# A Mamba block's convolution moved from diagonal matmuls to stacked, DMA-shifted copies on column tiles

## The chip, the cores and the metric

The kernel runs on one core of a Trainium2 chip. The core has five engines that work side by side, each through its own queue in program order: PE (TensorE, matmuls), DVE (VectorE), ACT (ScalarE), POOL (GpSimd) and SP (SyncE, which here only issues DMA transfers). The metric is the device time of one execution, in microseconds (us); lower is better.

## The reference

8192 rows x of 512 columns pass through two residual blocks. c and wmod give shift, scale and gate of each (sa, ca, ga, sb, cb, gb).

```python
h = _layernorm(x) * (1 + ca) + sa
xc, z = split(h @ W_in.T)                       # 1024 columns each
xc = silu(conv(xc, W_conv))                     # per column: 4 taps over the last 4 rows
dlt, Bm, Cm = split(xc @ W_xproj.T)             # 32, 16 and 16 columns
delta = softplus(dlt @ W_dt.T + b_dt)
# for each of 1024 columns d and 16 states n, over the 8192 rows in order:
s = exp(delta * A[d, n]) * s + delta * Bm[n] * xc[d];   y[d] += s * Cm[n]
x = x + ga * (((y + xc * D) * silu(z)) @ W_out.T)
h = _layernorm(x) * (1 + cb) + sb
x = x + gb * fp4_linear(silu(fp4_linear(h, w_gate)) * fp4_linear(h, w_up), w_down)
```

fp4_linear rounds both operands to a 4-bit grid, with one scale for each 16 values. All is float32.

## The kernel before

The rows are cut into 16 chunks of 512 (T), the 1024 inner columns into 8 blocks of 128 (ND), two blocks making one of four h groups. In the Mamba part columns lie on the partitions and rows run along the free axis.

**The scan loop.** The work is cut into 1024 slots: 16 chunks of 64 slots, one slot being one block and two states (`unit`, from L546). For each slot POOL multiplies delta times x by the rows of B into db (`make_db`, L521, two slots ahead), ACT takes the exponential into da (`make_da`, L534, one slot ahead, in PSUM), DVE runs the recurrence over 1024 elements (L559) and multiplies the result by the rows of C into hc (L577), or, in 5 of 16 slots, the scan writes hp and POOL does that product (L572). PE transposes the result into y (`add_up`, L438). Buffers: three db, two da, two hc and two hp.

**The rows of B and C** of two states, spread over all partitions, come by `load_bc` (L515): at the start of every second slot SP issues one 512 KB load of B and one of C, for the pair of slots that begins four slots later. Each has three buffers, so the load of C waits until the product with the rows three pairs back is done.

**The order of the rest** is written out by hand. `TABLE` (L589) gives for each step of chunk k a time in quarter-slots, counted from the chunk's first slot; a negative one lies in the chunk before. A quarter is one of four moments in `unit`: BEGIN (ahead of the slot), MID (between the two halves of da), GAP (ahead of make_db) and END. Every engine meets the work in this order, SP included. The convolution of chunk k thus runs during the slots of chunk k-1, in 15 passes (a few steps reach further back). Chunk 0's own convolution stands in the prologue, in steps called halves (L857 to L864, `on(h, ...)`), beside the FP4 quantization of w_gate and w_up, whose results go to DRAM.

**The convolution of one block d** has six steps:
- `conv_mm` (L285): four matmuls, 128x128 weights from w_in (the whole of W_in, resident in SBUF) against the normalized rows hT, into a PSUM tile cv;
- `conv_raw` (L297): ACT copies cv to raw, behind three carried columns, and keeps the last three for the next chunk;
- `conv_diag` (L290): ACT makes four diagonal 128x128 matrices, the identity times one tap each;
- `conv_taps` (L305): four matmuls of these against raw at four shifts, added up in cv;
- `conv_act` and `conv_out` (L312, L315): ACT takes tanh, DVE forms the block of xc.

cv comes from a pool of one PSUM bank in the loop, shared with the transposes of the norm (L267) and one of the two delta matmuls of a group. `x_proj` then makes 64 rows: 32 for delta, 16 of B, 16 of C; B and C go to DRAM for load_bc (L342). `prep_mm` (L358) makes delta of a group's two blocks from the 32 rows, one matmul of 32x128 weights each; `prep` is its softplus.

**The FFN** comes after the loop and shares only x and the quantized weights with it.

Of the kernel before, what the change touches and what calls it, by code (L numbers as in the profile page):

```python
# [108 lines left out]
def mamba_then_fp4_ffn(  # L109
# [60 lines left out]
    with ExitStack() as ma:  # L170
# [5 lines left out]
        cw = wp.tile([P, ND, 4], F32, tag="cw", name="cw")  # L176
# [8 lines left out]
        w_in = wi.tile([P, NK, 2 * DI], F32, tag="w_in", name="w_in")  # L185
        w_xp = wi.tile([P, ND, RK + 2 * NS], F32, tag="w_xp", name="w_xp")
        w_dt = wi.tile([RK, DI], F32, tag="w_dt", name="w_dt")
# [90 lines left out]
        def in_proj(k, o, ps):  # L278
            for f in range(NK):
                nc.tensor.matmul(  # L280
                    ps, lhsT=w_in[:, f, o : o + P], rhs=hT[k][:, f, :],
                    start=(f == 0), stop=(f == NK - 1),
                )

        def conv_mm(k, d):  # L285
            v = cv_tile(f"cv_{k}_{d}")
            in_proj(k, d * P, v)
            pend["v", k, d] = v

        def conv_diag(k, d):  # L290

            taps = s1.tile([P, 4, P], F32, tag="taps", name=f"taps_{k}_{d}")
            for i in range(4):
                nc.scalar.activation(taps[:, i, :], ident, AF.Copy, scale=cw[:, d, i : i + 1])  # L294
            pend["taps", k, d] = taps

        def conv_raw(k, d):  # L297
            v = pend["v", k, d]
# [4 lines left out]
            pend["raw", k, d] = raw  # L303

        def conv_taps(k, d):  # L305
            v, raw, taps = pend["v", k, d], pend["raw", k, d], pend.pop(("taps", k, d))
            for i in range(4):
                nc.tensor.matmul(  # L308
                    v, lhsT=taps[:, i, :], rhs=raw[:, i : i + T], start=(i == 0), stop=(i == 3)
                )  # L310
# [10 lines left out]
        def x_proj(k, half):  # L321
# [3 lines left out]
            for d in range(half * (ND // 2), (half + 1) * (ND // 2)):  # L325
                nc.tensor.matmul(
                    pb[: RK + 2 * NS, :], lhsT=w_xp[:, d, :], rhs=xcs[k, d],
# [9 lines left out]
        def x_proj_out(k, _=None):  # L337
            pb = pend.pop(("pb", k))
            dbc = s1.tile([RK + 2 * NS, T], F32, tag="dbc", name=f"dbc_{k}")
            nc.scalar.activation(dbc, pb[: RK + 2 * NS, :], AF.Copy)  # L340
            bc = scr.tile([2 * NS, T], F32, tag="bc", name=f"bc_{k}")
            nc.sync.dma_start(bc, dbc[RK:, :])  # L342
            dbcs[k], bcd[k], pend["pb", k] = dbc, bc, pb

        def first_mm(k, _=None):

            nc.tensor.matmul(
                pend["pb", k][:, :NS], lhsT=dbcs[k][:, 0:1].to_broadcast([RK + 2 * NS, P]),
                rhs=ident[: RK + 2 * NS, RK : RK + NS], start=True, stop=True,
# [8 lines left out]
        def prep_mm(k, h):  # L358
            for i in range(DH):
                d = h * DH + i  # L360
                pd = mm_tile(f"pd_{k}_{d}") if i % 2 else cv_tile(f"pd_{k}_{d}")
# [904 lines left out]
```

## Time and profile before

| | us |
|---|---|
| runs: median of 2 (lowest to highest) | 5705.88 (5698.72 to 5713.04) |
| profiled execution: span, first to last instruction | 5691.5 |
| until the first scan | 161 |
| scan loop, 161 to 3770 | 3609 |
| after it, the FFN | 1921.5 |

The profiled execution's own time outside its span is not listed; the median of the runs lies 14.4 us above its span.

How to read the lines: engine, source line, operation, then the tiles written and read; "x" is a count; then busy time and mean duration, or, in lines ordered by time, the start, the length and (in brackets) the idle time just before with what ended it. PE's float32 matmul of 128x512 appears as two records. In the list of waits a line has the waiting instruction, what it waited for, the sum in us, how often, and the longest. SPq is SP's queue of transfers, "to landing" the time from issue to the data's arrival.

### The profile page before, as it was taken

What the parts mean: (1) busy time and instruction counts of PE and PEld (TensorE: products, weight loads), DVE (VectorE), ACT (ScalarE), POOL (GpSimd) and SP (SyncE); (2) the same over time, 40 slices, a digit from 0 to 9 for tenths busy, and PEclk for the clock granted to TensorE, in tenths of its full rate; (3) what the DMA queues carried; (4) which work ended last, traced back from release to release, by engine and by line L of the source; (5) the groups of instructions that cost most, each with busy time, mean ns of one, the idle gap of its engine ahead of it and who ended that gap; (6) DMA issues with size and microseconds to landing.
All of it is one profiled execution on the core that took longest, in us unless ns stands there. A gap on an engine that the chain in (4) does not pass through costs nothing. (4 is left out here: it accounts for less than half of the span.)

```text
span 5691.5 us, 59773 instructions
## 1 busy us (share of the span) xinstructions
PE 5218.3 (92%) x19844; PEld 3065.0 (54%) x19844; DVE 4956.7 (87%) x4003; ACT 3214.2 (56%) x7319; POOL 4047.2 (71%) x2548
## 2 busy tenths in 40 slices
PE   7789889899899898998998988778999999999999
PEld 4556556556665565665666655543444444444444
DVE  7899999999999999999999999999687788878885
ACT  6677787777777777777777776643122222221221
POOL 4899999999999999999999999983222232223320
PEclk9899999999999999999999999889999999999999
DMA  5444454454445444544445444440100000000000
GB/s 183 150 158 157 156 160 162 154 169 153 161 154 164 153 161 156 163 163 160 157 158 160 155 160 151 160 165 17 34 27 23 27 31 32 23 24 31 33 13 15
DMA packets 221996, 659.50 MB, mean 116 GB/s; under 512 B 24915, under 2 KB 40403, under 8 KB 221686
## 3 DMA queue, kind: packets, MB, share of 16 engines
q1 hardware_dynamic: 221110, 654.63, 35.3%
q8 instruction: 156, 2.56, 0.2%
q14 instruction: 154, 1.26, 0.1%
q10 hardware_dynamic: 576, 1.05, 0.0%
HBM read 615.22 MB, written 40.38 MB: 115 GB/s over the span
## 5 line engine op out<-in xcount | busy, mean ns | idle before, releaser
L521 POOL TENSOR_TENSOR db<-bc,du 128x1022 f32<-128x1022 f32 x1024 | 2388.8, 2357 | 25.1 <-DVE da L559 20.9
L559 DVE TENSOR_TENSOR_SCAN da<-da,db 128x1024 f32<-128x1024 f32 x704 | 1610.0, 2287 | 100.3 <-ACT da L534 87.4
L534 ACT ACTIVATE da<-delta,na 128x512 f32<-128x512 f32 x2048 | 1412.4, 690 | 90.4 <-DVE hp L559 62.3
L577 DVE TENSOR_TENSOR hc<-da,bc 128x1024 f32<-128x1024 f32 x704 | 861.3, 1223 | 88.6 <-PE y L438 38.7
L438 PE MATMUL y<-ident,hc 128*128 128x128 f32 x5632 | 767.9, 287 | 154.1 <-DVE hc L577 98.3
L438 PEld LDWEIGHTS y<-ident,hc 128*128 128x128 f32 x5632 | 674.9, 148 | 330.5 <-issue 158.2
L97 POOL TENSOR_TENSOR xn<-xn,sc 128x1536 f32<-128x1536 f32 (+2 forms) x80 | 201.2, 2515 | 865.4 <-DVE xn L92 857.3
L559 DVE TENSOR_TENSOR_SCAN hp<-da,db 128x1024 f32<-128x1024 f32 x320 | 730.0, 2281 | 51.0 <-ACT da L534 45.3
L572 POOL TENSOR_TENSOR hp<-hp,bc 128x1024 f32<-128x1024 f32 x320 | 754.2, 2357 | 25.6
L1060 PE MATMUL pu<-xqT,wu 128*128 128x512 f32 x1408 | 637.3, 595 | 6.2 <-DVE ve L32 3.6
L1060 PE MATMUL pg<-xqT,wg 128*128 128x512 f32 x1408 | 638.1, 596 | 2.9 <-ACT g L1065 2.2
L83 ACT ACTIVATE a<-xn 128x512 f32<-128x512 f32 (+3 forms) x144 | 145.7, 1012 | 862.7 <-DVE xn L79 832.9
L1094 PE MATMUL po<-wd,hT 128*128 128x512 f32 x1408 | 608.7, 593 | 2.0 <-DVE hT L1080 2.0
L280 PE MATMUL cv<-hT,w_in 128*128 128x512 f32 x1024 | 490.2, 624 | 32.9 <-ACT hT L273 16.1
L412 PE MATMUL pz<-w_in,hT 128*128 128x256 f32 x2048 | 495.4, 398 | 26.6 <-DVE z L427 21.6
L308 PE MATMUL cv<-raw,taps 128*128 128x512 f32 x1024 | 469.3, 601 | 5.4 <-ACT taps L294 5.1
L474 PE MATMUL po<-w_o,xc 128*128 128x512 f32 x1024 | 457.4, 592 | 0.2 <-ACT xc L467 0.2
L412 PEld LDWEIGHTS pz<-w_in,hT 128*128 128x128 f32 x2048 | 404.1, 202 | 95.3 <-DVE z L427 26.0
L1060 PEld LDWEIGHTS pu<-xqT,wu 128*128 128x128 f32 x1408 | 267.9, 191 | 342.2 <-issue 323.2
L1094 PEld LDWEIGHTS po<-wd,hT 128*128 128x128 f32 x1408 | 267.9, 190 | 339.8 <-issue 330.6
L557 ACT ACTIVATE state<-da 128x2 f32<-128x2 f32 x703 | 118.0, 168 | 588.7 <-DVE hc L577 586.9
L1060 PEld LDWEIGHTS pg<-xqT,wg 128*128 128x128 f32 x1408 | 266.6, 191 | 327.3 <-issue 319.8
(125 smaller groups left out, 6696.6 us busy)
## 6 DMA issues: line engine op xcount, KB each, us to landing
bc<-bc SPq DMA_DIRECT2D x1024, 512.0 KB, 4.3
x<-in_x_dram SPq DMA_DIRECT2D x64, 256.0 KB, 4.7
h<-in_x_dram SPq DMA_DIRECT2D x64, 256.0 KB, 2.8
x<-mo SPq DMA_DIRECT2D x64, 256.0 KB, 2.9
out_dram<-x SPq DMA_DIRECT2D x64, 256.0 KB, 2.0
mo<-po SPq DMA_DIRECT2D x60, 256.0 KB, 2.2
w_in<-in_w_inT_dram SPq DMA_DIRECT2D x2, 2048.0 KB, 9.8
wm<-in_wmod_dram SPq DMA_DIRECT2D x8, 512.0 KB, 4.5
```

The costliest lines, as they stand in the source:

```text
L280: nc.tensor.matmul(ps, lhsT=w_in[:, f, o : o + P], rhs=hT[k][:, f, :], start=(f == 0), stop=(f == NK - 1),)
L308: nc.tensor.matmul(v, lhsT=taps[:, i, :], rhs=raw[:, i : i + T], start=(i == 0), stop=(i == 3))
L412: nc.tensor.matmul(pz[:, b, :], lhsT=hT[k][:, f, t0 : t0 + P], rhs=w_in[:, f, o : o + DH * P], start=(b == 0 and f == 0), stop=(f == NK - ...
L438: nc.tensor.matmul(y[:, j, i * P : (i + 1) * P], lhsT=src[:, j * P : (j + 1) * P], rhs=ident, start=start and j % 2 == 0, stop=stop, is_tr ...
L474: nc.tensor.matmul(pend["po", k, j], lhsT=xcs[k, d][:, j * P : (j + 1) * P], rhs=w_o[:, d, :], start=(d == 0), stop=(d == ND - 1),)
L521: nc.gpsimd.tensor_tensor(db[:, :, 1:], bct[slot // DH, 0][:, :, 1:], dus[k, h, i][:, 1:].unsqueeze(1).to_broadcast([P, GN, T - 1]), ALU.mult,
L534: nc.scalar.activation(pend["da", slot][:, q, :], deltas[k, h][:, i, :], AF.Exp, scale=na[:, d, n : n + 1])
L559: nc.vector.tensor_tensor_scan(flat(to), flat(da), flat(db), 0.0, ALU.mult, ALU.add)
L572: nc.gpsimd.tensor_tensor(to, to, c_rows, ALU.mult)
L577: nc.vector.tensor_tensor(hc, hs, c_rows, ALU.mult)
L1060: nc.tensor.matmul(ps, lhsT=wt[:, k, f * P : (f + 1) * P], rhs=xqT[n][:, k, :], start=(k == 0), stop=(k == NK - 1),)
L1094: nc.tensor.matmul(pos[j], lhsT=hTs[n, c][:, o : o + P], rhs=wd[:, f0 + i, :], start=(f0 + i == 0), stop=(f0 + i == NF - 1),)
```

## The change

The four shifts are no longer taken by reading raw at four offsets on PE. `conv_raw` now also issues 16 transfers from SBUF to SBUF, each 32 partitions of 512 values: shift i of the 32-column group g goes to partitions 32i to 32i+31 of a tile rows. `conv_taps` then needs one matmul for each group of 32 columns, with weights of 128x32 that hold four 32x32 diagonals, each on its own column tile of PE and into its own 32 partitions of a fresh cv tile. These weights (taps) are made once, by DVE in `neg_a`, and `conv_diag` is gone. cw is loaded by 16 small transfers in the order that this needs.

The half of W_in for x is not resident any more: `load_w` brings 128 columns (256 KB) for each block, into two buffers. The delta rows are made twice (w_xp has 96 columns), and the two delta matmuls of a group stand on two row tiles (partitions 0 to 31 and 32 to 63).

In the compiled instruction lists each of the 16 copies waits on SP for the transfer issued eight transfers earlier to have landed, as other transfers did before; nothing else on SP is reordered, the loads of B and C stay where they were. Times of the convolution's steps in TABLE change as shown; all other times stay.

```diff
-        cw = wp.tile([P, ND, 4], F32, tag="cw", name="cw")
+        taps = wp.tile([P, ND, 4, 32], F32, tag="taps", name="taps")
...
-        w_in = wi.tile([P, NK, 2 * DI], F32, tag="w_in", name="w_in")
-        w_xp = wi.tile([P, ND, RK + 2 * NS], F32, tag="w_xp", name="w_xp")
-        w_dt = wi.tile([RK, DI], F32, tag="w_dt", name="w_dt")
+        w_z = wi.tile([P, NK, DI], F32, tag="w_z", name="w_z")
+        w_xp = wi.tile([P, ND, 2 * RK + 2 * NS], F32, tag="w_xp", name="w_xp")
+        w_dt = wi.tile([2 * RK, ND // 2, P], F32, tag="w_dt", name="w_dt")
+        wxp = ma.enter_context(tc.tile_pool(name="wx", bufs=2))
...
+        def load_w(k, d):
+            wx = wxp.tile([P, NK, P], F32, tag="wx", name=f"wx_{k}_{d}")
+            nc.sync.dma_start(
+                wx, w_inT[:, d * P : (d + 1) * P].rearrange("(k p) n -> p k n", p=P)
+            )
+            pend["wx", k, d] = wx
...
-        def conv_diag(k, d):
-
-            taps = s1.tile([P, 4, P], F32, tag="taps", name=f"taps_{k}_{d}")
-            for i in range(4):
-                nc.scalar.activation(taps[:, i, :], ident, AF.Copy, scale=cw[:, d, i : i + 1])
-            pend["taps", k, d] = taps
-
         def conv_raw(k, d):
-            v = pend["v", k, d]
+            v = pend.pop(("v", k, d))
             raw = s2.tile([P, T + 3], F32, tag="raw", name=f"raw_{k}_{d}")
             nc.scalar.activation(raw[:, 3 : T + 3], v, AF.Copy)
             nc.scalar.activation(raw[:, 0:3], tail[:, d, :], AF.Copy)
             nc.scalar.activation(tail[:, d, :], v[:, T - 3 : T], AF.Copy)
-            pend["raw", k, d] = raw
+
+            rows = s1.tile([P, 4, T], F32, tag="rows", name=f"rows_{k}_{d}")
+            for i in range(4):
+                for g in range(4):
+                    nc.sync.dma_start(
+                        rows[32 * i : 32 * (i + 1), g, :], raw[32 * g : 32 * (g + 1), i : i + T]
+                    )
+            pend["raw", k, d], pend["rows", k, d] = raw, rows
 
         def conv_taps(k, d):
-            v, raw, taps = pend["v", k, d], pend["raw", k, d], pend.pop(("taps", k, d))
-            for i in range(4):
+            v = pend["v", k, d] = cv_tile(f"cx_{k}_{d}")
+            rows = pend.pop(("rows", k, d))
+            for g in range(4):
                 nc.tensor.matmul(
-                    v, lhsT=taps[:, i, :], rhs=raw[:, i : i + T], start=(i == 0), stop=(i == 3)
+                    v[32 * g : 32 * (g + 1), :], lhsT=taps[:, d, g, :], rhs=rows[:, g, :],
+                    start=True, stop=True, tile_position=(0, 32 * g),
                 )
...
+                r = slice(i * RK, (i + 1) * RK)
                 nc.tensor.matmul(
-                    pd, lhsT=w_dt[:, d * P : (d + 1) * P], rhs=dbcs[k][:RK, :], start=True, stop=True
+                    pd, lhsT=w_dt[r, h, :], rhs=dbcs[k][r, :], start=True, stop=True,
+                    tile_position=(i * RK, 0),
                 )
...
             "conv": (
-                (-251, -247, -246, -242, -231, -229), (-228, -221, -220, -213, -207, -205),
-                (-201, -196, -191, -188, -184, -182), (-174, -170, -164, -162, -159, -149),
-                (-139, -133, -130, -128, -122, -120), (-119, -114, -113, -108, -105, -97),
-                (-89, -85, -81, -78, -71, -66), (-59, -58, -55, -54, -49, -46),
+                (-290, -251, -247, -233, -231, -229), (-262, -228, -222, -209, -207, -205),
+                (-231, -201, -196, -182, -180, -178), (-203, -173, -169, -154, -152, -149),
+                (-174, -139, -133, -122, -120, -118), (-140, -116, -112, -100, -98, -96),
+                (-119, -91, -87, -70, -68, -66), (-88, -63, -60, -42, -40, -38),
             ),
...
-            "conv": (conv_mm, conv_raw, conv_diag, conv_taps, conv_act, conv_out),
+            "conv": (load_w, conv_mm, conv_raw, conv_taps, conv_act, conv_out),
...
-                nc.vector.tensor_scalar(cw, cw, 0.5, None, ALU.mult)
+                fold = mp.tile([P, 32], F32, tag="fold", name="fold")
+                nc.vector.tensor_reduce(
+                    fold, ident.rearrange("p (b c) -> p c b", c=32), AX.X, ALU.add
+                )
+                nc.vector.scalar_tensor_tensor(
+                    taps.rearrange("p d g c -> p (d g) c"),
+                    cw.rearrange("p d g -> p (d g)").unsqueeze(2).to_broadcast([P, 4 * ND, 32]),
+                    0.5, fold.unsqueeze(1).to_broadcast([P, 4 * ND, 32]), ALU.mult, ALU.mult,
+                )
...
-            nc.sync.dma_start(w_in[:, :, :DI], w_inT[:, :DI].rearrange("(k p) n -> p k n", p=P))
-            nc.sync.dma_start(cw, w_conv)
+            load_w(0, 0)
+            load_w(0, 1)
+            cw = mp.tile([P, ND, 4], F32, tag="cw", name="cw")
+            for i in range(4):
+                for g in range(4):
+                    nc.sync.dma_start(
+                        cw[32 * i : 32 * (i + 1), :, g], w_conv[32 * g : 32 * (g + 1), :, i]
+                    )
...
                 on(h, conv_mm, 0, d)
                 on(h + 1, conv_raw, 0, d)
-                on(h + 1, conv_diag, 0, d)
+                on(h, load_w, 0, d + 2) if d + 2 < ND else None
                 on(h + 2, conv_taps, 0, d)
```

## The prediction

> **What bounds the kernel now.** I read the page's first part, then busy time by stage, then the waits of the engines that are nearly full. The page:
>
> ```profile
> span 5691.5 us, 59773 instructions
> ...
> PE 5218.3 (92%) x19844; PEld 3065.0 (54%) x19844; DVE 4956.7 (87%) x4003; ACT 3214.2 (56%) x7319; POOL 4047.2 (71%) x2548
> ```
>
> Four engines share the lead, so these shares are an average over stages. The stages are: until the first scan (161 us), the scan loop (to 3770 us), the FFN. Columns: length, then busy us of PE, weight load, DVE, ACT, POOL, then clock, DMA share, GB/s.
>
> ```profile
> 0.00:161.00 161.00, 122.03 (x387) 68.25 (x388) 107.22 (x108) 101.56 (x230) 75.63 (x60) 0.96 0.57 181
> 161.00:3770.00 3609.00, 3211.58 (x14867) 2145.80 (x14867) 3339.72 (x2102) 2690.15 (x6567) 3409.96 (x2102) 0.94 0.49 159
> 3770.00:5691.50 1921.50, 1884.72 (x4593) 850.94 (x4591) 1509.79 (x1794) 422.51 (x523) 561.65 (x390) 0.99 0.09 30
> ```
>
> The FFN is PE's (1885 of 1921 us) and the change does not touch it. In the loop POOL is busy 94%, DVE 93%, PE 89%, ACT 75%. One chunk of 64 slots takes 225.5 us (3609/16), of which DVE works 209 us and POOL 213 us: what any relief of PE or ACT can give is the 12 to 17 us a chunk that DVE and POOL stand idle. What ends DVE's idle time in the loop:
>
> ```profile
> DVE da L559 <- ACT da L534: 87.4, 58, 3.8
> DVE hp L559 <- ACT da L534: 45.3, 15, 4.4
> DVE hc L577 <- PE y L438: 38.7, 34, 1.9
> DVE z L450 <- PE y L438: 25.5, 16, 2.5
> ```
>
> So DVE waits 133 us for ACT and 64 us for PE, 12 us a chunk. No wait for a transfer is in the list: the loads of B and C rows come in time today. Walking one chunk slot by slot (the one from 1295.7 us), the waits for ACT stand in few places: 1.5 us at slot 10, about 1.4 at slots 15 and 16, 2.7 at slot 42, 0.6 at slot 44, 3.3 at slot 61. Slots 15, 42 and 61 follow prep (softplus, two table loads) and stay. Slot 10 is the convolution's:
>
> ```profile
> 1324.62 0.60 ACT L300 ACTIVATE raw<-cv 128x512 f32<-128x512 f32 x1 [0.74 <-PE cv L280]
> 1325.41 1.27 ACT L294 ACTIVATE taps<-ident,cw 128x128 f32<-128x128 f32 x4
> ...
> 1327.97 1.42 ACT L534 ACTIVATE da<-delta,na 128x512 f32<-128x512 f32 x2 [1.15 <-DVE hp L559]
> ```
>
> The copies and the four diagonals sit between two scans' da; the scan at 1329.47 then waited 1.54 us.
>
> **The change, part by part.**
>
> *Diagonals go.* Four ACT operations a block, 1.27 us as they run together. Most of it lies in ACT's idle 25%. Visible are slots 10 and 44: 2.1 us a chunk gained, 2.6 if the neighbours 15 and 16 lose something too, 1.6 if only slot 10 does.
>
> *Taps on column tiles.* A 128x512 matmul is two records here; eight run in 3.44 us in the chain of waits. Today's four taps matmuls thus take 3.44 us. Four column tiles take 0.86 us if they run side by side, 3.44 if not. Column tiles are not in the trace. Either way it lies under DVE: none of DVE's waits for PE (slots 15, 16, 55) stands at a taps matmul. I take 0 for both ends, the shorter one as cover for the stalls below. Delta's row tiles (two matmuls, 1.72 to 0.86 us) give nothing: ACT takes the first result after 0.86 us in both cases. The 96-row dbc costs ACT what the 64-row one did: a copy of 64x512 took 0.58 us, one of 128x512 0.58 to 0.60.
>
> The Trainium skill (TensorEngine Tiling (Array Packing), "Key Properties" and "Theoretical Speedup") promises up to 4x for 32 columns and says that changing the tiling mode drains the engine. No row here shows a drain. By the first the estimate is 2.6 us of PE a block, by the second less; both vanish under DVE.
>
> *Copies and weights on SP.* A block adds 17 issues: one 256 KB load of W_in, 24 to 39 quarter-slots ahead of its matmul, into a buffer long free (nobody waits), and 16 SBUF copies of 32x512 (64 KB). The same shape, to DRAM, is in the trace:
>
> ```profile
> L342 SPq DMA_DIRECT2D bc<-dbc x16: 317/318/342, 150.6 to 3528.8; - x16
> DMA to landing us min/median/max: 1.6/1.6/1.7
> ```
>
> A lone issue takes 0.32 us. Issued back to back, the second and later take 0.42 (records of h and x loads), start to start 0.47 us; lone ones start to start 0.37; in the crowded opening about 0.56. I take 0.47, since sixteen in a row are like the former: 7.5 us of SP a block (ends 5.9 and 9.0), then 1.7 us to land. In the instruction list each copy also waits for the transfer eight issues before it: 8 x 0.47 = 3.8 us is longer than 1.7, so that costs nothing inside the row. Bytes: 128 blocks x 1.25 MB are some 46 GB/s more on 159, DMA share 0.49 to about 0.63, no bound.
>
> The Trainium skill (DMA: Bandwidth & Descriptors, "Anatomy of one DMA" and "Rules for kernel authors") gives 2.0 us fixed plus bytes over 436 GB/s, here 2.15 us as an estimate, and says to coalesce: transfers under 64 KB are mostly overhead. The row above lands in 1.6 us. Paid one after another the rule would make 34 us a block, 10 slots, against the 2.75 to 4.5 that the table leaves; the overlapped issue of bc loads speaks for the smaller price.
>
> *What is queued behind the 16 copies* is the next load of B and C rows (L515), issue to landing 4.3 us, and POOL's db needs it. I placed each block at its new moment in the same chunk. Six of eight have room (late by 0.5 us at most). Two do not. Block 5's raw, at slot 36:
>
> ```profile
> 1418.72 0.60 ACT L300 ACTIVATE raw<-cv 128x512 f32<-128x512 f32 x1 [0.43 <-PE cv L280]
> 1419.22 0.20 ACT L301 ACTIVATE raw<-tail 128x3 f32<-128x3 f32 x1
> ```
>
> ```profile
> 1422.38 6.98 POOL L521 TENSOR_TENSOR db<-bc,du 128x1022 f32<-128x1022 f32 x3
> ...
> 1431.90 6.96 POOL L521 TENSOR_TENSOR db<-bc,du 128x1022 f32<-128x1022 f32 x3
> ```
>
> ```profile
> 1432.71 2.29 DVE L559 TENSOR_TENSOR_SCAN da<-da,db 128x1024 f32<-128x1024 f32 x1
> ...
> 1436.24 2.28 DVE L559 TENSOR_TENSOR_SCAN hp<-da,db 128x1024 f32<-128x1024 f32 x1
> ```
>
> Copies from 1419.4 to 1426.9; B's load lands at 1431.2. The third db of the first line (slot 40) began at 1427.0: 4.2 us late. It would end at 1433.5, its scan stood at 1432.7 (0.8 lost); the next db, 1431.90 plus 4.2, ends at 1438.5 where its scan wants 1437.0 (1.4 lost). Block 3, raw ready at 1371.6, likewise: the load lands at 1383.5, db of slot 26 began at 1380.85, 2.65 late; the scan had 1.6 of room, so 1.0 is lost, and 0.75 more where later slots have 0.9 to 1.2 of room. Sum 4.0 us a chunk; with 0.37 us an issue 0.75; with 0.56 us 7.0.
>
> *Taps wait for the copies.* Landed 10.2 us after raw was reached (11.6 at block 0, behind a C load). PE comes to taps 8.0 us (block 4), 8.9 to 9.7 (blocks 0, 1, 5) and over 11 us after it: up to 6 us of PE stall a chunk, behind it the y matmuls, which free hc's buffers; PE has 25 us idle a chunk, more with shorter taps. Block 4's tanh makes ACT wait 1.3 us. I take 0.8 us a chunk for DVE, ends 0 and 1.5.
>
> Loop: 4.0 + 0.8 - 2.1 = +2.7 us a chunk, 15 chunks (the last prepares none): +40 us. Ends: 0.75 + 0 - 2.6 = -1.9, -28 us; 7.0 + 1.5 - 1.6 = +6.9, +104 us.
>
> *The prologue.* The eight convolution blocks of chunk 0 are a chain: PE does the next block's matmul after this block's taps, and copies now stand between. From raw's end to taps was 2.3 us at block 0 (48.0 to 50.3), with 1.27 of diagonals inside. Now 16 x 0.56 + 2 = 11 us, minus 2.6 for shorter taps: about +6 us a block if nothing covers it, 48 us for eight. Block 0's copies also queue behind the loads of w_o, w_xp and w_dt. Cover: PE stands idle 39 of 161 us, and the FP4 chain of POOL and DVE runs beside it; but the chain's spacing (12 us a block) is already three quarters of what the new one needs. Reloading W_in there makes SP wait for the matmul two blocks earlier, which is part of the same chain. The new taps tile costs DVE one pass over 128x1024 (1.2 us) for the 1.7 us that scaling cw took. Sixteen 4-byte-element loads of cw ahead of the second weight tile cost some 3 us. I take +45, ends 0 and 85.
>
> Sum on the profiled execution: 5691.5 + 40 + 45 = 5776.5. Its span is 14.4 us under the median of the runs, 5705.9, and I put that around it: 5791 us.
>
> **The rivals.**
>
> *Starved scan.* Issues cost 0.56 us in the loop as well, db is late at blocks 0 and 1 too, and the prologue gets no cover: 5706 + 104 + 85 = 5895. For it: POOL at 94% cannot catch up. Against: outside the opening, back-to-back issues stand at 0.47.
>
> *Relief wins* (the other side). If issues start 0.37 us apart, db at slots 26 and 40 loses only 0.75 us a chunk and the diagonals' gap decides: 5706 - 28 = 5678 with a covered prologue. The point is about 0.43 us an issue in the loop. For it: 32 rows are a quarter of the 128 rows of the loads that gave 0.47. Against: small loads of 128 rows also took 0.42.
>
> *Copies paid one by one.* If each copy's 1.6 us came after the other's, 26 us a block, PE would stall some 15 us in 120 blocks: 7500 us. Against: bc loads are issued 0.4 us apart and land in 4.3.
>
> *The change doesn't do what it says*: column tiles run one after another. Taps keep 3.44 us, ACT's tanh waits up to 2.6 us longer at block 4: at most +39 us, 5830.
>
> **How the numbers follow.** Forecast (5720 to 5820) 0.50; starved scan, with serial tiles, 0.28; relief 0.20; one by one 0.02. The range takes the ends of the sum: 5678 to 5895. 2% of 5706 is 114 us, about what a measurement of this kernel can tell from no change: faster needs 5592, below even the relief case, 0.01; slower needs 5820, the second and fourth cases, 0.30; same 0.69.
>
> **What would show it.** DMA rows among the releasers of POOL's db, near slots 26 and 40; SP issues of the copies 0.47 us apart; DVE's wait at slot 10 gone; the first scan near 205 us instead of 161; taps matmuls waiting for copies at blocks 0 and 4; the FFN at 1921 us. I am wrong if the chunk takes under 225 us, or if the prologue keeps its length.

## The result, and the profile after

The changed kernel takes 6162.57 us (median of 2 runs, 6161.5 to 6163.65) against 5705.88 (5698.72 to 5713.04): ratio 1.080, 95% interval 1.076 to 1.085. It is 8% slower; forecast were 5791 us, with a range of 5678 to 5895. By stages, from the two profiled executions:

| us | before | after | predicted step |
|---|---|---|---|
| first scan begins | 161.1 | 234.3 (+73.2) | +45 |
| one chunk, mean of the 15 that prepare the next one | 226.2 | 252.6 (+26.4) | +2.7 |
| last chunk (it prepares none) | 212.3 | 211.4 | 0 |
| FFN, from the loop's end | 1924.5 | 1927.8 | 0 |
| span | 5691.5 | 6161.8 (+470) | +85 |

The loop has 15 x 26.4 = 396 of the 470 us. The page of the changed kernel:

```profile
span 6161.8 us, 62677 instructions
...
PE 5153.0 (84%) x19844; PEld 2995.7 (49%) x19844; DVE 4978.8 (81%) x4004; ACT 3070.9 (50%) x6807; POOL 4044.1 (66%) x2548
```

No engine has noticeably more to do than before: PE is busy 65 us less, ACT 143 less (the diagonals), DVE and POOL are within 0.5%. The loss is waiting. Busy time by stage of the changed kernel (length, PE, weight load, DVE, ACT, POOL, clock, DMA share, GB/s):

```profile
0.00:234.25 234.25, 122.94 (x385) 62.57 (x386) 106.31 (x109) 93.74 (x198) 74.40 (x60) 0.80 0.56 162
234.25:4234.00 3999.75, 3141.68 (x14857) 2079.20 (x14855) 3355.09 (x2099) 2554.08 (x6086) 3407.08 (x2098) 0.90 0.59 182
4234.00:6161.80 1927.80, 1888.34 (x4604) 853.95 (x4604) 1517.44 (x1797) 423.07 (x524) 562.62 (x392) 0.99 0.09 30
```

In the loop DVE fell from 93% busy to 84%, POOL from 94% to 85%. The list of waits of the changed kernel names the new ones:

```profile
POOL db L530 <- DMA bc<-bc: 376.5, 108, 9.4
...
ACT raw L320 <- PE cx L314: 260.3, 81, 13.8
...
PE cx L314 <- DMA rows<-raw: 168.7, 56, 17.4
...
PE pt L268 <- DVE xc L325: 157.3, 14, 11.9
...
ACT x L234 <- DMA x<-in_x_dram: 127.7, 18, 12.0
DVE da L568 <- POOL db L530: 114.2, 47, 5.4
DVE xc L325 <- ACT raw L320: 114.2, 50, 14.5
DVE hc L586 <- PE y L447: 107.2, 63, 5.7
```

Before, of these eight only the last was there in any size (38.7 us), and the loop had a single wait for a transfer, of 0.3 us. Read four things: POOL waits for B rows; PE's taps matmuls wait for the copies, ACT's tanh (L320) for these, DVE's xc (L325) for tanh; ACT waits for an x tile of the next norm; and PE's norm transposes (L268) wait, 14 times, 11 us, for DVE's xc. What counts in the end is DVE, the fullest engine: its idle time grew from 14.1 to 39.4 us a chunk, nearly all of the 26.4. The trace puts most of it in four places: db (0.2 to 9.1 us a chunk), xc (0 to 5.0), slot 54 (0 to 5.9) and slot 55 (1.6 to 5.7).

SP's side, first the copies, then (a second look at the same kernel) the loads of B and C: count, issue ns as min/median/max, and the time to landing.

```profile
L305 SPq DMA_DIRECT2D rows<-raw x2048: 507/589/1843, 63.4 to 3978.9; - x187
...
DMA to landing us min/median/max: 1.9/2.0/6.2
```

```profile
L524 SPq DMA_DIRECT2D bc<-bc x1024: 319/382/1610, 225.4 to 4221.5; - x171
...
DMA to landing us min/median/max: 3.3/5.7/9.9
```

The copies start 0.633 us apart (median over the loop), not 0.47: 10.2 us of SP for a block (mean), not 7.5. A load of B or C lands after 5.7 us, not 4.3. The end of one chunk, in order of time, from block 7's raw on:

```profile
1431.29 10.94 SPq L305 DMA_DIRECT2D rows<-raw  x16
...
1443.40 0.42 SPq L226 DMA_DIRECT2D x<-in_x_dram  x1
...
1446.43 4.63 POOL L530 TENSOR_TENSOR db<-bc,du 128x1022 f32<-128x1022 f32 x2 [3.46 <-DMA bc<-bc]
...
1449.88 0.63 ACT L234 ACTIVATE x<-x 128x512 f32<-128x512 f32 x1 [8.62 <-DMA x<-in_x_dram]
...
1453.37 2.29 DVE L568 TENSOR_TENSOR_SCAN hp<-da,db 128x1024 f32<-128x1024 f32 x1 [6.97 <-ACT da L543]
...
1454.29 0.58 ACT L320 ACTIVATE raw<-cx 128x512 f32<-128x512 f32 x1
...
1456.29 1.11 PE L268 MATMUL pt<-ident,xh 128*128 128x128 f32 x4 [11.48 <-DVE xc L325]
...
1464.57 1.22 DVE L586 TENSOR_TENSOR hc<-da,bc 128x1024 f32<-128x1024 f32 x1 [5.08 <-PE y L447]
```

SP is busy with copies for 11 us; then loads of B, C and x follow. POOL waits 3.5 us for B. ACT waits 8.6 us for the x tile, with the da of the next scan behind it in its queue, so DVE waits 7.0. PE stands 11.5 us before the norm's transpose, because the one PSUM bank is held by block 7's convolution until DVE's xc has read it; the y matmuls are behind it, so DVE waits again, 5.1 us. The two are linked: block 7's taps had ended at 1444.8 us, but its tanh (L320) stands behind the x tile on ACT and runs only at 1454.29.

### The profile page after: what moved, and what is told of

It is laid out like the page before. It is cut to its first block, busy times and chain, and to the rows that moved or that the text cites. A ratio compares the mean times of both kernels' runs of the same rounds, so it can differ in the third digit from the quotient of the medians.

```text
span 6161.8 us, 62677 instructions
## 1 busy us (share of the span) xinstructions
PE 5153.0 (84%) x19844; PEld 2995.7 (49%) x19844; DVE 4978.8 (81%) x4004; ACT 3070.9 (50%) x6807; POOL 4044.1 (66%) x2548
## 5 line engine op out<-in xcount | busy, mean ns | idle before, releaser
L530 POOL TENSOR_TENSOR db<-bc,du 128x1022 f32<-128x1022 f32 x1024 | 2388.4, 2355 | 456.0 <-DMA bc<-bc 376.5
L568 DVE TENSOR_TENSOR_SCAN da<-da,db 128x1024 f32<-128x1024 f32 x704 | 1611.4, 2289 | 240.8 <-POOL db L530 114.2
L447 PE MATMUL y<-ident,hc 128*128 128x128 f32 x5632 | 809.2, 295 | 365.7 <-DVE hc L586 269.0
L447 PEld LDWEIGHTS y<-ident,hc 128*128 128x128 f32 x5632 | 695.5, 152 | 585.2 <-DVE hc L586 345.7
L421 PE MATMUL pz<-w_z,hT 128*128 128x256 f32 x2048 | 519.2, 411 | 51.8 <-DVE z L436 28.9
L290 PE MATMUL cv<-hT,wx 128*128 128x512 f32 x1024 | 498.0, 632 | 59.0 <-ACT delta L380 28.9
L483 PE MATMUL po<-w_o,xc 128*128 128x512 f32 x1024 | 481.4, 618 | 0.3 <-ACT xc L476 0.2
L421 PEld LDWEIGHTS pz<-w_z,hT 128*128 128x128 f32 x2048 | 417.3, 209 | 131.8 <-DVE z L436 34.0
L314 PE MATMUL cx<-rows,taps 128*32 128x512 f32 x1024 | 314.0, 694 | 173.4 <-DMA rows<-raw 168.7
```

Source lines behind the costliest of these rows:

```text
L290: nc.tensor.matmul(v, lhsT=wx[:, f, :], rhs=hT[k][:, f, :], start=(f == 0), stop=(f == NK - 1))
L314: nc.tensor.matmul(v[32 * g : 32 * (g + 1), :], lhsT=taps[:, d, g, :], rhs=rows[:, g, :], start=True, stop=True, tile_position=(0, 32 * g),)
L421: nc.tensor.matmul(pz[:, b, :], lhsT=hT[k][:, f, t0 : t0 + P], rhs=w_z[:, f, o : o + DH * P], start=(b == 0 and f == 0), stop=(f == NK - 1 ...
L447: nc.tensor.matmul(y[:, j, i * P : (i + 1) * P], lhsT=src[:, j * P : (j + 1) * P], rhs=ident, start=start and j % 2 == 0, stop=stop, is_tr ...
L483: nc.tensor.matmul(pend["po", k, j], lhsT=xcs[k, d][:, j * P : (j + 1) * P], rhs=w_o[:, d, :], start=(d == 0), stop=(d == ND - 1),)
L530: nc.gpsimd.tensor_tensor(db[:, :, 1:], bct[slot // DH, 0][:, :, 1:], dus[k, h, i][:, 1:].unsqueeze(1).to_broadcast([P, GN, T - 1]), ALU.mult,
```

## The experiments

Every run has the same 64 slots of scan in a chunk. The tables give the median time, the first scan and the mean chunk. "No copies" means that taps read hT. Chunk and first scan are those of one profiled execution, which can lie up to some 17 us from the median of the runs (the last kernel below: 5986.8 against 6003.9), or 1 us a chunk; smaller differences say nothing.

### What the copies cost

These four were timed once each; the kernel before took 5713.3 us beside them.

**No copies.**

```diff
-            rows = s1.tile([P, 4, T], F32, tag="rows", name=f"rows_{k}_{d}")
-            for i in range(4):
-                for g in range(4):
-                    nc.sync.dma_start(
-                        rows[32 * i : 32 * (i + 1), g, :], raw[32 * g : 32 * (g + 1), i : i + T]
-                    )
...
-                    v[32 * g : 32 * (g + 1), :], lhsT=taps[:, d, g, :], rhs=rows[:, g, :],
+                    v[32 * g : 32 * (g + 1), :], lhsT=taps[:, d, g, :], rhs=hT[k][:, g, :],
```

> The 16 copies of each block are left out and the taps matmuls read another tile (hT), so the convolution is not the reference's; column tiles, row tiles, reloaded weights and the new table all stay. Theory A (the copies cost it all, through SP and the waits on them): first scan back to 161 us give or take 15, chunk 222 to 228 us instead of 253, total 5670 to 5760 us. Rival B (the tiling modes, the reloading of W_in or the new table cost it): chunk stays above 240 us, total above 5950 us.

**Copies that nobody reads.**

```diff
-            pend["raw", k, d], pend["rows", k, d] = raw, rows
+            pend["raw", k, d] = s1.tile([P, T], F32, tag="th", name=f"th_{k}_{d}")
...
-                    v[32 * g : 32 * (g + 1), :], lhsT=taps[:, d, g, :], rhs=rows[:, g, :],
+                    v[32 * g : 32 * (g + 1), :], lhsT=taps[:, d, g, :], rhs=hT[k][:, g, :],
```

> The 16 copies are issued as in the changed kernel, but nothing reads them: the taps matmuls read hT and tanh goes to a tile of its own, so the convolution is not the reference's. What stays is SP's time in front of the loads of B, C and x. Theory A1 (the loads behind the copies come late): POOL still waits 25 to 30 us a chunk for B rows, chunk 245 to 250 us, prologue shorter by some 40 us, total about 6030 us (5980 to 6090). Theory A2 (the waits of PE and ACT for the copies themselves are the cost): chunk about 228 us, total about 5750 us.

**Copies of half the bytes.**

```diff
-                        rows[32 * i : 32 * (i + 1), g, :], raw[32 * g : 32 * (g + 1), i : i + T]
+                        rows[32 * i : 32 * (i + 1), g, : T // 2], raw[32 * g : 32 * (g + 1), i : i + T // 2]
...
-                    v[32 * g : 32 * (g + 1), :], lhsT=taps[:, d, g, :], rhs=rows[:, g, :],
+                    v[32 * g : 32 * (g + 1), :], lhsT=taps[:, d, g, :], rhs=rows[:, g, : T // 2].unsqueeze(1).to_broadcast([P, 2, T // 2]),
```

> 16 copies as before, but of half the columns each (32x256, 32 KB); the taps matmuls read the half twice, so the convolution is not the reference's. If an issue has a price of its own (0.63 us each whatever the bytes), SP spends 10.2 us a block as in the changed kernel and the total stays within 40 us of 6162. If the price goes by bytes or by the load on the transfer engines, issues shrink towards 0.45 us and the total falls to about 5930 us or lower.

**Half the copies.**

```diff
-                for g in range(4):
+                for g in range(2):
...
-                    v[32 * g : 32 * (g + 1), :], lhsT=taps[:, d, g, :], rhs=rows[:, g, :],
+                    v[32 * g : 32 * (g + 1), :], lhsT=taps[:, d, g, :], rhs=rows[:, g % 2, :],
```

> Eight copies a block instead of 16 (full width; groups 2 and 3 of the columns read those of 0 and 1, so the convolution is not the reference's). The bytes are those of the half-width run. If the number of issues is the cost, SP spends 5.1 us a block: in the placement of the prediction that leaves blocks 3 and 5 late by 0.2 to 2 us, chunk about 228 us, prologue about 195 us, total about 5780 us (5720 to 5860). If the cost goes by bytes, it equals the half-width run.

| | us | first scan | chunk |
|---|---|---|---|
| the changed kernel | 6162.6 | 234.3 | 252.6 |
| no copies | 5842.1 | 157.6 | 236.2 |
| copies unread | 6110.4 | 200.0 | 251.5 |
| half the bytes | 6113.6 | 227.1 | 249.6 |
| half the copies | 5901.7 | 195.4 | 237.7 |

The price goes by issue: with half the bytes the copies still start 0.633 us apart and 49 us come back; with half the copies 261 of the 320 us come back. No copies gave 5842, neither theory's value: about 129 us (5842 - 5713) have nothing to do with the copies. Half the copies missed its value too (5902, expected up to 5860), in which these had no place. And leaving the reads away changes the chunk by 1 us only, where 16 of its 26 us hang on the copies. That could mean that waiting for the copies is free and SP's queue is everything. The next groups show that it means something else.

Column tiles can be seen without the copies' pace (PE in the run without copies, start and length of a block's eight records):

```profile
1361.40 1.06 PE L307 MATMUL cx<-hT,taps 128*32 128x512 f32 x8
```

Eight records of 0.6 us in 1.06 us, four of them starting within 0.02 us: the four tiles run side by side. Before, a block's taps took 3.60 us (median of 128). The Trainium skill (TensorEngine Tiling (Array Packing), "Theoretical Speedup") gives up to 4x for 32 columns; here it is 3.4. The change of tiling has a small price, which the prediction could not see: after a y matmul the first taps matmul starts 0.20 us later (median), where it was 0.11 in the kernel before, and the next matmul without tiles starts 0.52 us after the last of the taps has started, where it was 0.43. In the changed kernel itself the median of a block's taps is 2.84 us, because the data comes one copy at a time: in the chunk shown above, the weights of the four groups are loaded at 1441.77, 1442.40, 1443.08 and 1443.76 us.

### What is left without the copies

**No copies, and the convolution's moments of the kernel before** (load_w stays where the change put it).

```diff
-    (-290, -251, -247, -233, -231, -229), (-262, -228, -222, -209, -207, -205),
+    (-290, -251, -247, -242, -231, -229), (-262, -228, -221, -213, -207, -205),
...
-    (-119, -91, -87, -70, -68, -66), (-88, -63, -60, -42, -40, -38),
+    (-119, -89, -85, -78, -71, -66), (-88, -59, -58, -54, -49, -46),
```

> The changed kernel without its 16 copies (the taps matmuls read hT, so the output is not the reference's), and with the convolution's steps at the moments they had in the kernel before; W_in is still reloaded, the taps are on column tiles, delta on row tiles. It separates what is left of the loss without the copies (5842 against 5713 us, 10 us a chunk). If the new moments cost it (block 7's bank of PSUM is still held when the next chunk's first norm transposition asks for it): 5705 to 5750 us, chunk 226 to 228. If the tiles or the reload cost it: over 5800, chunk over 234.

**The kernel before with the new moments.**

```diff
-    (-251, -247, -246, -242, -231, -229), (-228, -221, -220, -213, -207, -205),
+    (-251, -247, -246, -233, -231, -229), (-228, -222, -221, -209, -207, -205),
...
-    (-89, -85, -81, -78, -71, -66), (-59, -58, -55, -54, -49, -46),
+    (-91, -87, -86, -70, -68, -66), (-63, -60, -59, -42, -40, -38),
```

> The kernel before, whole, with nothing but the convolution's moments of the changed kernel (diagonals one quarter of a slot after raw). If the new moments cost the 10 us a chunk: 5800 to 5870 us, with PE waiting at the norm's transpose (L268 of after) for DVE's xc. If tiles or reload cost it: 5690 to 5740.

**No copies, block 7 earlier.**

```diff
-    (-88, -63, -60, -42, -40, -38),
+    (-88, -63, -60, -45, -44, -43),
```

> The changed kernel without its copies (taps read hT; output not the reference's), and block 7's taps, tanh and output moved from quarter slots -42, -40, -38 to -45, -44, -43, so that the one PSUM bank is free before the next chunk's first norm transposition asks for it at -42. Theory (the bank held at slot 54 is a part of what the new moments cost): DVE's idle time at slot 55 goes from 4.5 us back to about 1.6, the chunk from 236.5 to about 233.5, the kernel from 5842 to about 5797 us (5770 to 5815). Rival (the norm's transposition only waits where PE would have waited anyway): 5830 to 5850.

**No copies, only the taps matmuls at their old moments.**

```diff
-    (-290, -251, -247, -233, -231, -229), (-262, -228, -222, -209, -207, -205),
+    (-290, -251, -247, -242, -231, -229), (-262, -228, -222, -213, -207, -205),
...
-    (-119, -91, -87, -70, -68, -66), (-88, -63, -60, -42, -40, -38),
+    (-119, -91, -87, -78, -68, -66), (-88, -63, -60, -54, -40, -38),
```

> The changed kernel without its copies (taps read hT; output not the reference's), with the taps matmuls of each block at the moments of the kernel before (4 to 12 quarter slots earlier) and all other moments new. Theory (PE comes to the late taps behind y matmuls, and tanh and DVE's xc, two quarter slots behind each other, then make DVE wait in its own order at slots 6, 7, 26, 27 and 43): DVE's idle time there, 5 us a chunk in the run without copies, goes; the kernel at 5740 to 5800 us. Rival (taps are not late, the tanh and xc moments or block 7's bank cost all of it): 5820 to 5850.

**The kernel before without its diagonals.**

```diff
-            taps = s1.tile([P, 4, P], F32, tag="taps", name=f"taps_{k}_{d}")
-            for i in range(4):
-                nc.scalar.activation(taps[:, i, :], ident, AF.Copy, scale=cw[:, d, i : i + 1])
-            pend["taps", k, d] = taps
+            if (k, d) == (0, 0):
+                pend["one"] = s1.tile([P, 4, P], F32, tag="taps", name="taps")
+                for i in range(4):
+                    nc.scalar.activation(pend["one"][:, i, :], ident, AF.Copy, scale=cw[:, d, i : i + 1])
...
-            v, raw, taps = pend["v", k, d], pend["raw", k, d], pend.pop(("taps", k, d))
+            v, raw, taps = pend["v", k, d], pend["raw", k, d], pend["one"]
```

> The kernel before, with the four diagonals made once and used for all blocks (the taps' values are wrong for all other blocks; PE's matmuls are as they were). It measures by itself what the prediction took for the diagonals, 2.1 us a chunk at slots 10 and 44: 5705 - 34 = 5670 us if that holds; 5700 or more if slot 10's wait is DVE's and ACT's order at that slot and no matter of the diagonals.

| | us | ratio to before, 95% | first scan | chunk |
|---|---|---|---|---|
| no copies, old moments | 5725.3 | 1.003 (1.002 to 1.005) | 158.9 | 228.3 |
| before, new moments | 6027.2 | 1.057 (1.055 to 1.059) | 159.6 | 248.7 |
| no copies, block 7 earlier | 5785.8 | 1.013 (1.012 to 1.015) | 157.5 | 232.3 |
| no copies, old taps moments | 5804.9 | 1.016 (1.015 to 1.018) | 156.4 | 233.8 |
| before, no diagonals | 5719.7 | 1.002 (1.001 to 1.003) | 156.8 | 228.6 |

The tiles, the 96 rows for delta and the reload of W_in, with the diagonals gone, cost 15 us together (5725 - 5711): nearly free, as predicted. The new moments cost the rest: 236.2 - 228.3 = 7.9 us a chunk. They put taps, tanh and xc two quarter slots (some 1.8 us, from 226.2/256 a quarter) behind one another; before, tanh came 3 to 11 quarters behind taps. Waits of the kernel before with these moments:

```profile
ACT raw L313 <- PE cv L308: 347.2, 90, 9.5
...
DVE xc L318 <- ACT raw L313: 163.9, 61, 6.1
...
PE pt L267 <- DVE xc L318: 72.6, 15, 4.9
```

With the old moments the first two of these were 4.7 and 5.8 us. PE reaches taps late, behind the output projection and y matmuls; ACT is then held at tanh and DVE at xc, and their scan work queues behind. Block 3 in one chunk of this kernel, in order of time:

```profile
1487.63 1.97 PE L438 MATMUL y<-ident,hc 128*128 128x128 f32 x8 [3.85 <-DVE hc L577]
...
1489.39 8.94 PE L474 MATMUL po<-w_o,xc 128*128 128x512 f32 x16
...
1499.04 3.60 PE L308 MATMUL cv<-raw,taps 128*128 128x512 f32 x8
...
1503.31 0.69 DVE L318 SCALAR_TENSOR_TENSOR xc<-raw,cv 128x512 f32<-128x512 f32 x1 [5.91 <-ACT raw L313]
```

A part of this lateness is PE's clock. PE stands idle for 3.85 us, until 1487.63; the granted clock is 0.50 from 1486.4 to 1493.2 us, and the first matmuls of L474 start 0.85 us apart, the later ones 0.43. Over 15 chunks of the kernel before and of this one (length, PE, weight load, DVE, ACT, POOL, clock, DMA share, GB/s):

```profile
161.10:3554.80 3393.70, 3056.58 (x14106) 2029.89 (x14104) 3136.31 (x1979) 2560.62 (x6274) 3203.26 (x1978) 0.95 0.49 158
```

```profile
159.60:3890.60 3731.00, 3201.13 (x14106) 2114.95 (x14104) 3149.76 (x1979) 2547.29 (x6274) 3209.95 (x1977) 0.91 0.43 144
```

The same 14106 records of PE take 145 us more, 9.6 us a chunk. How much of the 317 us that the moments cost here (6027 - 5711) goes by way of the clock is not shown. In the run without copies they cost 117 (5842 - 5725). That run has the shorter taps, but also no diagonals and a second tile for taps, so what of the difference the shorter taps bring is open.

A second part is the PSUM bank. In the run without copies, and then with block 7 earlier as well:

```profile
PE pt L268 <- DVE xc L318: 124.3, 14, 9.4
...
DVE hc L579 <- PE y L440: 109.5, 57, 5.6
```

```profile
PE pt L268 <- DVE xc L318: 76.6, 14, 5.6
...
DVE hc L579 <- PE y L440: 71.4, 59, 3.4
```

DVE's idle time at slot 55 falls from 5.5 to 2.0 us and the chunk by 3.9. Taps at their old moments take away DVE's idle time at slots 6, 7, 26 and 27, but 2.0 us at slot 43 stay; the chunk falls by 2.4, a little less than expected (5804.9, expected 5740 to 5800). The two together, 6.3 of the 7.9 us, were not run together.

The diagonals bring nothing: without them the kernel before is not faster but 0.2% slower.

### Two losses in the same time

**B's loads one window earlier**, the kernel otherwise whole.

```diff
-                        load_bc(slot // DH + 2)
+                        load_bc(slot // DH + 2, 1)
+                    if slot % DH == 0 and slot // DH + 3 < NSLOT // DH:
+                        load_bc(slot // DH + 3, 0)
```

The second argument is 0 for B and 1 for C; ahead of the loop three loads of B and two of C are issued, where it was two of each.

> The changed kernel, whole, but each load of B rows is issued one window of four slots earlier, after the C load of the window and ahead of the copies that follow (buffers as they were). Theory (the loop loses because B's loads stand behind 16 copies on SP; POOL's db waits 29 us a chunk for them): those waits fall by more than half, db is in time, and the chunk falls from 253 us to 240 to 245, the kernel to 5950 to 6050 us; the waits for x loads and for the convolution's PSUM bank stay. Rival (the loop loses because the transfers themselves are slow, whatever stands ahead of them): POOL's waits move to other slots, the chunk stays over 249, the kernel over 6100.

**The same, and copies unread.** The edit is that diff with the one of the run "copies that nobody reads".

> The changed kernel with its copies issued and read by nobody (taps read hT; output not the reference's) and B's loads issued one window earlier. Leaving the reads away alone gave 6110, B ahead alone 6120. Theory (two losses lie in the same time, each covers the other: DVE waits either for db behind late B loads, or for xc behind taps that wait for their copies): with both away the chunk falls to 237 to 242, the kernel to 5880 to 5980 us (no copies at all gave 5842; the prologue keeps 40 us of its loss). Rival (the two add up singly): 6110 + 6120 - 6162 = 6068 or more.

**And the x tile ahead of the copies, block 7 earlier.**

```diff
-                (-308, -300, -294, -291, -289, -289, -280),
+                (-318, -300, -294, -291, -289, -289, -280),
...
-    (-88, -63, -60, -42, -40, -38),
+    (-88, -63, -60, -45, -44, -43),
```

> The changed kernel with its copies issued and read by nobody (taps read hT; output not the reference's), B's loads one window earlier (5921 us so far), and two more things that stand in line moved: the load of the next norm's second x tile goes from quarter slot -308 to -318, ahead of block 7's copies, and block 7's taps, tanh and output to -45, -44, -43. Theory (DVE's 5.3 us at slot 54 are ACT waiting for that x load behind the copies, its 4.0 us at slot 55 the PSUM bank): both go, chunk 239 to 229 to 233, kernel 5760 to 5840 us. Rival (x's load is late because transfers are slow beside the copies, wherever it is issued): slot 54 keeps over 3 us, kernel over 5870.

**The same with the copies read**: the whole computation again.

> The changed kernel, whole, copies read, with the same three moves (B's loads and the x tile ahead of the copies, block 7 three to five quarter slots earlier). It prices what is left: taps waiting for copies, in PE's order, and tanh and xc behind them. Theory: chunk 250 (B ahead alone) to 240 to 244, kernel 5980 to 6040 us, DVE idle only at xc (slots 6, 26, 34, 39) and where the kernel before idled. Rival (with reads, the time given back at slots 54 and 55 is lost again at block 7's own copies, which have less time now): chunk 247 or more, kernel over 6080.

| | us | ratio to before, 95% | first scan | chunk |
|---|---|---|---|---|
| the changed kernel | 6162.6 | 1.080 (1.076 to 1.085) | 234.3 | 252.6 |
| copies unread (timed once) | 6110.4 | | 200.0 | 251.5 |
| B ahead | 6120.3 | 1.073 (1.071 to 1.075) | 230.9 | 249.7 |
| B ahead, copies unread | 5921.1 | 1.037 (1.035 to 1.040) | 199.6 | 238.5 |
| B, x ahead, block 7 earlier, unread | 5813.8 | 1.019 (1.017 to 1.020) | 197.5 | 231.7 |
| B, x ahead, block 7 earlier | 6003.9 | 1.052 (1.049 to 1.054) | 231.5 | 241.1 |

The second and third rows give back 1.1 (within the spread) and 2.9 us a chunk, both together 14.1. Each loss lies under the other: DVE waits either for db, because B came late, or for xc, because taps waited for their copies. My theory for B ahead alone (a chunk of 240 to 245) was wrong by this. Waits with B ahead:

```profile
ACT raw L320 <- PE cx L314: 306.8, 83, 13.6
PE cx L314 <- DMA rows<-raw: 194.1, 63, 17.3
DVE xc L325 <- ACT raw L320: 187.6, 65, 13.6
...
ACT x L234 <- DMA x<-in_x_dram: 117.5, 18, 12.4
...
POOL db L530 <- DMA bc<-bc: 69.5, 33, 4.8
```

POOL's wait for B fell from 376.5 to 69.5 us as it should; the wait of DVE for xc grew from 114.2 to 187.6 in its place. With the copies unread as well, little is left of either (DVE waits 0.4 us a chunk for db and 2.7 for xc, most of it at slot 26), and the chunk falls. The waits of that run (B ahead, copies unread), and then with x ahead and block 7 earlier:

```profile
PE pt L268 <- DVE xc L324: 200.8, 14, 15.2
...
ACT x L234 <- DMA x<-in_x_dram: 122.2, 19, 12.1
...
DVE hc L585 <- PE y L446: 88.9, 58, 5.5
```

```profile
DVE hc L585 <- PE y L446: 75.7, 59, 3.2
...
PE pt L268 <- DVE xc L324: 72.9, 14, 5.6
...
ACT x L234 <- DMA x<-in_x_dram: 19.4, 4, 11.6
```

The x tile and the bank go, with 6.8 us a chunk. At 231.7 the chunk is where it is without any copies (232.3 with block 7 earlier): all 16 copies are still issued and cost the loop nothing, as long as nobody waits for them and nothing urgent stands behind them. Reading them then costs 9.4 us a chunk (241.1; some 10 by the medians of the runs, an estimate: 190 us less 34 of the prologue, over 15 chunks), in these waits of the last kernel:

```profile
ACT raw L320 <- PE cx L314: 356.3, 95, 13.5
...
DVE xc L325 <- ACT raw L320: 194.1, 71, 14.9
PE cx L314 <- DMA rows<-raw: 194.1, 66, 17.3
```

In the loop DVE then idles at xc in slots 6, 26, 34 and 39, 2.4 to 2.6 us each.

### Another way for the rows

**One store to DRAM, four loads back**, with B ahead and block 7 earlier.

```diff
-            rows = s1.tile([P, 4, T], F32, tag="rows", name=f"rows_{k}_{d}")
-            for i in range(4):
-                for g in range(4):
-                    nc.sync.dma_start(
-                        rows[32 * i : 32 * (i + 1), g, :], raw[32 * g : 32 * (g + 1), i : i + T]
-                    )
+            xr = scr.tile([P, T + 3], F32, tag="xr", name=f"xr_{k}_{d}")
+            nc.sync.dma_start(xr, raw)
...
+        def conv_rows(k, d):
+            xr = pend.pop(("xr", k, d)).rearrange("(g p) t -> p g t", p=32)
+            rows = pend["rows", k, d] = s1.tile([P, 4, T], F32, tag="rows", name=f"rows_{k}_{d}")
+            for i in range(4):
+                nc.sync.dma_start(rows[32 * i : 32 * (i + 1)], xr[:, :, i : i + T])
```

conv_rows stands six quarter slots after conv_raw; scr is in DRAM.

> The changed kernel, whole, by another way: raw goes to a DRAM buffer in one store, and six quarter slots later four loads bring the four shifted copies (32 partitions x 4 x 512 each) back, 5 issues a block for 16; B's loads one window ahead; block 7's taps, tanh and output three to five quarter slots earlier. Theory (the price is by issue): SP 3 us a block for 10, chunk 235 to 242, prologue 185 to 205, kernel 5860 to 5960 us, still slower than before because the moments and the tanh chain remain. Rival (the second trip through DRAM lands too late for the taps): chunk over 248, kernel over 6080.

It took 6240 us (ratio 1.093, 1.091 to 1.095), first scan 248.2, chunk 257.4: slower than the copies. The loads of rows in this kernel, four a block:

```profile
L310 SPq DMA_DIRECT2D rows<-xr x512: 302/424/1362, 66.2 to 4057.8; - x171
...
  PE cx L316: 502.9, 90
...
DMA to landing us min/median/max: 2.9/6.5/10.1
```

The issues are cheap (0.42 us, five in all), but two trips stand behind each other: the loads go out 2.7 to 8.3 us after raw (medians by block) and land 6.5 us later; PE begins taps 10.1 to 17.6 us after raw, no sooner than with the copies (9.8 to 17.6), and waits for the rows 502.9 us, against 194.1 with the copies and B ahead. The count of issues is a price only as far as something is queued behind them; here the landing decides.

No run here points to a version that beats the kernel before. The nearest is the run without copies at the old moments, 1.003, and it does not compute the convolution. Not run were the copies at the old moments, and the copies issued from another engine than SP.

## Why the prediction was wrong

It failed in the loop's sum, "+2.7 us a chunk", measured +26.4. Taken apart along one path of runs (the order matters, since the losses cover each other): B's loads behind the copies 2.9 (252.6 to 249.7), the x tile and the bank 8.6 (to 241.1), waiting for the copies 9.4 (to 231.7), the remaining new moments 3.4 (to 228.3, copies gone as well), tiles and reload 2.1 (to 226.2). The last is 1.0 by the medians of the runs (15 us over 15 chunks).

- **"I take 0.47"** for an issue: 0.633, above the upper end of 0.56. The row was of another kind (loads from DRAM over 128 partitions). 10.2 us of SP a block for 7.5.
- **"Six of eight have room", sum 4.0.** POOL waits for B at more places than the two that were named, 25 us a chunk (376.5/15), most of it at slots 39, 25, 7, 53 and 12. But DVE loses time for db almost only where the working had put it, at slots 26, 40 and 41: 8.3 of 9.1 us a chunk. Mechanism and place were right, the size was half. A row of copies takes 10.2 us for 7.5 and the load lands in 5.7 us for 4.3, which makes it 4.1 us later still: 4.2 + 4.1 = 8.3 us, and POOL waits 8.2 at slot 39. It is not the whole loss: taken away alone, it gives back 2.9 us, since the waits for xc stand behind it.
- **"What is queued behind the 16 copies is the next load of B and C rows."** The next norm's x tile is queued there too (block 7), ACT waits for it, with da behind. Not in the working at all; it stands behind the 5.9 us of DVE at slot 54.
- **The moments in TABLE were costed at nothing.** Moved were not only copies: taps, tanh and xc stand closer, and block 7 holds the bank when the norm asks for it. In the kernel before these moments alone cost 317 us. A whole edit was left out of the sum, and its part about the bank was to be read from the diff: out at -38, the norm's transpose at -298, which is -42 one chunk on.
- **"I take 0.8 us a chunk"** for taps waiting: 9.4 once no load hides it. I had 25 us of PE's idle time as cover; but PE waits in its own order, and ACT's tanh and DVE's xc wait behind it.
- **"Visible are slots 10 and 44: 2.1 us a chunk gained"**. Slot 10 costs DVE 1.49 us a chunk with the diagonals and 1.49 without them (means), and the run without them gained nothing. The line that the prediction showed says it: da there waits 1.15 us for DVE's hp, not for ACT's own diagonals.
- **Column tiles, row tiles, the reload at 0**: right (1.003 for all three together). The tiles do run side by side.
- **The prologue, +45 (0 to 85)**: +73, inside the ends. 42 us come from the issues alone (copies unread: 200.0 against 157.6), 34 from waiting for them. Two small terms were mis-sized: the 16 loads of cw held SP for 15.3 us, not 3, and the pass that makes taps took 2.9 us, not 1.2. No run takes them out; the run without copies has both, and its first scan is no later than before.
- **The FFN unchanged**: right.

The rival *starved scan* had the right direction and one of the two main mechanisms; no rival had the moments.

## What to carry to other kernels

In a schedule written by hand, every moved moment is an edit of its own: ask for each what is now next to what on the in-order engines, and who asks next for the buffer it holds. A row of transfers is priced by what is queued behind it on the issuing engine and by who waits for its last piece; when both hold the same engine, taking away one shows almost nothing, so take away both before calling either harmless. A relief on engines that are off the critical path (here ACT's diagonals and PE's taps) is worth what the slots' waits say, and here that was nothing; but PE, made to stand, came back at half its clock, and this lengthens a wait further.

## What the runs showed of the hardware

- A copy from SBUF to SBUF of 32 partitions takes SP 0.59 us to issue (0.633 start to start), for 64 KB and for 32 KB alike (both medians), while one store of 257 KB from 128 partitions took 0.32 us and a load of 256 KB into 32 partitions 0.42.
- The copies land in 2.0 us (1.9 for half the bytes). The Trainium skill (DMA: Bandwidth & Descriptors, "Anatomy of one DMA") puts nearly all of a small transfer's time into a fixed 2.0 us. It says so of transfers issued by GpSimd; these are issued by SP, and the number agrees. In a row it is not paid 16 times: from the first issue to the last landing a row took 11.5 us (median).
- PE's granted clock fell to 0.50 within a wait of 3.85 us and stayed there for 6.8 us, and its 128x512 matmul records then started 0.85 us apart for 0.43 (the kernel before with new moments).
- The granted clock and the traffic of the copies do not explain what the copies cost in the loop. With all copies issued and unread, and all else ahead of them, a stretch of the loop has clock 0.90, DMA share 0.64 and 199 GB/s; without copies, with block 7 earlier, 0.93, 0.49 and 163. Both have the same chunk. Length, busy times, clock, DMA share and GB/s of the two, in that order:

```profile
300.00:3700.00 3400.00, 2846.82 (x13835) 1937.54 (x13834) 3069.74 (x1937) 2373.84 (x5684) 3131.18 (x1936) 0.90 0.64 199
```

```profile
300.00:3700.00 3400.00, 2746.22 (x13801) 1867.26 (x13800) 3062.71 (x1928) 2369.43 (x5668) 3127.28 (x1931) 0.93 0.49 163
```
